# The last stage's down projection by seven half-width products instead of eight full ones, with the next token group's transposes ahead of it

## The chip, the core and the metric

The kernel runs on one core of one Trainium2 chip. The metric is the device time of one execution in microseconds. A profile of one execution comes with it: for every engine (PE is TensorE, PEld its weight loads, DVE is VectorE, ACT is ScalarE, POOL is GpSimd, SP is SyncE, whose queue issues most transfers) it has each instruction's start, duration, and what it waited for.

## The reference, cut to what matters

Two transformer layers on 2048 tokens (2 sequences of 1024) of width 512, in float32. Each of four sublayers is normalised before and after and added to the stream `x`. Only the fourth is touched:

```python
def _L1_ffn_ref(x, w_gate, w_up, w_down):          # widths: 512 -> 2048 -> 512
    h = silu(einsum('bsh,hi->bsi', x, w_gate)) * einsum('bsh,hi->bsi', x, w_up)
    h_sparse = _sparsify_2to4(h)                   # of each 4 neighbours the 2 largest in size stay
    return einsum('bsi,ih->bsh', h_sparse, w_down)

x = x + _layernorm(_L1_ffn_ref(_layernorm(x), w_gate, w_up, w_down))
```

The first sublayer is a small attention over heads of the same token, the second a feed-forward layer with ternary weights, the third causal attention with rotary positions.

## The kernel before

The stream `x_sb` stays on chip: 16 tiles of 128 tokens by 512. The fourth sublayer, called the last stage here, is the code from L1104 to L1304. It goes over the tokens in NG = 4 groups `g` of GW = 512 tokens (four tiles, `GT = 4`), and in each group over NS = 4 slices `S` of the 2048 hidden columns, 512 columns each. A slice is two units `u` (L1192).

**A unit** (`f1_unit`, L1128) computes 256 hidden columns of gate and of up for the group's 512 tokens. Each of the two is a matrix product cut into 2 x 2 blocks and done with seven block products in place of eight (Strassen's scheme in Winograd's form). A block product is two matmuls of 128 x 128 weights against 128 x 256 moving values, so a unit has 2 x 7 x 2 = 28 matmuls. They stand in four phases: eight matmuls, eight, eight, four. ACT copies finished block products out of PSUM, DVE adds others (`add`, L1125); banks come from a ring of eight (`ring8`, L88), six for each unit, so the first bank of a unit is one that a DVE `add` of the unit before has to leave. Between the phases DVE does the preceding unit's work: `multiply` (L1175, two 128x1024 products, after ACT's sigmoid), and a share of the preceding slice's `choice` (L1205: twelve comparisons, additions and masked products that apply the two-of-four rule; `choose(2)`, `choose(3)`, `choose(2)` take the next so many of them).

The token side of the scheme needs sums of blocks of the transposed, normalised tokens; `sides` (L936) makes them in four DVE instructions. The weight side is made on POOL by `derive` (L919) during the first group, four POOL instructions of 128x256 for each of gate and up in each of eight units; all seven blocks are written to DRAM (`kept`), and the later groups load them back whole (`load_unit`, L900, 896 KB each).

**The down projection** (`f1_out`, L1239) of a 128-token tile is 16 matmuls, 128x128 of the hidden values against 128x512 rows of `wd`, in one PSUM bank. `wd` (4 MB) is loaded once, in four pieces during the first group, and stays. A tile's result is normalised and added to the stream (`f1_store`, L1247, through `ln_residual`, L209: statistics on DVE, square root on ACT, scaling on DVE, addition and the store on POOL).

The order of the work in the last stage is written out by hand for PE, ACT, DVE and SP; POOL's is left to the framework. At the end of a group stand: the last unit's sigmoid, `multiply` and the last slice's `choice`; the next group's normalisation (`f1_norm`, L1252); slices 0 to 2 of the first two tiles' down projection, then their slice 3; the next group's transposes (`f1_xT`, L1262, 16 PE transposes) and `sides`; then the other two tiles.

## Time and profile before

| | us |
|---|---|
| median of 3 runs | 1582.63 |
| the runs | 1582.63, 1578.23, 1583.45 |
| profiled execution, its own time | 1577.97 |
| its span, first to last instruction | 1575.8 |
| last stage's first matmul starts | 954.22 |
| last stage's last matmul ends | 1567.39 |

In the profile's rows "f32" matmuls stand as two instructions each, so the 256 down-projection matmuls appear as x512 and a unit's 28 as 56. A "mean ns" is one instruction's duration with its pipeline; back to back they start closer together than that, so the time that a series takes is read from starts. A "windows" row gives, for a stretch, the busy time of each engine and the number of instructions in brackets.

### The profile page before, as it was taken

Reading aid. Unit: us, or ns where it says so; the run is one execution under the profiler, and the core shown is the slowest. Engines: PE = TensorE matmul, PEld = TensorE weight load, DVE = VectorE, ACT = ScalarE, POOL = GpSimd, SP = SyncE. Lnnn points to the kernel's source line nnn. Section 1 sums busy time; section 2 is a strip of 40 time slices with the busy share of each in tenths; the row PEclk is TensorE's granted clock in tenths of the full one; section 3 lists DMA queues with packets and bytes.
Section 4 is the critical chain, followed back from the end, with each engine's and each line's share of the span. In section 5 each row is a group of like instructions: output and inputs, shape, how many; then the busy total and the mean of one; then the engine's idle time right before and its main releaser. Section 6 shows DMA issues by size and latency. Waiting matters only on the chain.

```text
span 1575.8 us, 19277 instructions
## 1 busy us (share of the span) xinstructions
PE 1493.5 (95%) x6614; PEld 977.9 (62%) x6614; DVE 952.7 (60%) x2221; ACT 740.2 (47%) x1876; POOL 304.2 (19%) x382
## 2 busy tenths in 40 slices
PE   6999999999688998998999999999999999999997
PEld 3558787877455544444444447874887488648863
DVE  6886356433676677657667636984377346824761
ACT  4243344322286767896787973440343044204420
POOL 1112335232201211114212015811000100010001
PEclk9999999999879999998899999999999999999999
DMA  7200001011552322225120005760233024203200
GB/s 287 74 1 0 1 1 44 11 34 34 131 135 60 88 50 55 61 54 177 51 54 1 1 1 179 276 233 21 101 141 139 20 109 173 100 21 146 95 1 27
DMA packets 59290, 125.51 MB, mean 80 GB/s; under 512 B 8116, under 2 KB 29622, under 8 KB 59192
## 3 DMA queue, kind: packets, MB, share of 16 engines
q1 hardware_dynamic: 54552, 104.09, 21.4%
q0 software_dynamic: 3584, 18.88, 3.1%
q10 hardware_dynamic: 1056, 1.31, 0.2%
q8 instruction: 52, 0.85, 0.2%
q14 instruction: 46, 0.38, 0.1%
HBM read 94.90 MB, written 29.36 MB: 79 GB/s over the span
## 4 chain that ended last, share of the span: by engine, by line
PE 46%; issue 32%; DVE 9%; ACT 9%; POOL 3%; DMA 1%; SPq 0%; POOLq 0%; ACTq 0%; DVEq 0%
PE ph L366 9%; ACT junk L757 5%; PE po L385 5%; PE pq L243 3%; PE pst L818 3%; PE pq L483 3%; PE psc L742 3%; PE po L847 3%; DVE mxs L753 3%; PE py L863 3%; ACT pT L831 2%; PE po L1242 2%; PE pb_g L1120 1%; PE pb_u L1120 1%; PE pkv L488 1%
## 5 line engine op out<-in xcount | busy, mean ns | idle before, releaser
L753 DVE TENSOR_REDUCE mxs<-psc 128x1 f32<-128x512 f32 (+3 forms) x384 | 196.3, 551 | 90.0 <-PE psc L748 51.0
L757 ACT ACTIVATE junk<-psc,mxs 128x512 bf16<-128x512 f32 (+3 forms) x384 | 222.9, 638 | 26.3 <-DVE mxs L753 18.2
L1242 PE MATMUL po<-wd,h 128*128 128x512 f32 x512 | 220.9, 592 | 0.0
L831 ACT ACTIVATE pT<-pst 128x512 f32<-128x512 f32 (+3 forms) x384 | 160.9, 560 | 54.0 <-PE pst L825 53.6
L366 PE MATMUL ph<-xTg,w 128*128 128x512 f32 x704 | 170.2, 395 | 1.9 <-DVE xTg L356 0.9
L1242 PEld LDWEIGHTS po<-wd,h 128*128 128x128 f32 x512 | 97.0, 190 | 119.3 <-issue 116.5
L742 PE MATMUL psc<-k,q 128*128 128x512 f32 (+3 forms) x384 | 144.0, 448 | 15.5 <-ACT junk L757 9.3
L366 PEld LDWEIGHTS ph<-xTg,w 128*128 128x128 f32 x704 | 132.3, 189 | 30.2 <-DVE xTg L356 1.2
L818 PE MATMUL pst<-q,k 128*128 128x512 f32 (+3 forms) x384 | 125.4, 417 | 11.3 <-ACT junk L757 9.8
L742 PEld LDWEIGHTS psc<-k,q 128*128 128x128 f32 x384 | 75.7, 208 | 78.3 <-ACT pT L831 33.7
L214 POOL TENSOR_TENSOR x_sb<-x_sb,tmp_f 128x512 f32<-128x512 f32 x16 | 20.2, 1260 | 508.4 <-DVE tmp_f L194 508.4
L833 POOL TENSOR_SCALAR_AFFINE_SELECT pT<-pT 128x256 f32<-128x256 f32 x128 | 52.1, 414 | 294.9 <-ACT pT L831 292.9
L818 PEld LDWEIGHTS pst<-q,k 128*128 128x128 f32 x384 | 69.0, 199 | 58.3 <-ACT junk L757 35.3
L757 ACT ACTIVATION_READ_ACCUMULATOR junk<-psc,mxs 128x1 f32 x384 | 100.7, 263 | 0.0
L177 ACT ACTIVATE rs_f<-mv_f,eps_t 128x1 f32<-128x1 f32 (+1 forms) x20 | 5.9, 295 | 200.6 <-DVE mv_f L175 200.6
L847 PE MATMUL po<-pT,v 128*32 128x512 f32 (+3 forms) x768 | 91.6, 513 | 1.6 <-POOL pT L833 1.1
L375 POOL TENSOR_TENSOR hl<-h,hl 128x512 fp32r<-128x512 f32 x44 | 57.1, 1298 | 169.5 <-ACT hl L374 169.5
L385 PE MATMUL po<-w,hl 128*128 128x512 f32 x352 | 87.4, 391 | 1.9 <-DVE tmp L194 1.9
L372 DVE TENSOR_TENSOR h<-h,ph 128x512 f32<-128x512 f32 x44 | 30.0, 684 | 96.4 <-PE ph L366 95.4
L1176 DVE TENSOR_TENSOR gate<-gate,ab 128x1024 f32<-128x1024 f32 x32 | 40.6, 1270 | 77.1 <-ACT ab L1173 77.1
L174 DVE BATCH_NORM_STATS2 st_f<-po 128x6 f32<-128x512 f32 x16 | 11.2, 699 | 108.8 <-PE po L1242 108.8
L385 PEld LDWEIGHTS po<-w,hl 128*128 128x128 f32 x352 | 65.8, 188 | 17.0 <-DVE tmp L194 3.6
(236 smaller groups left out, 2731.6 us busy)
## 6 DMA issues: line engine op xcount, KB each, us to landing
w<-kept SPq DMA_DIRECT2D x48, 896.0 KB, 5.2
q<-dq SPq DMA_DIRECT2D x64, 256.0 KB, 5.0
kept<-w POOLq DMA_DIRECT2D x16, 896.0 KB, 6.6
dq<-hl SPq DMA_DIRECT2D x32, 320.0 KB, 3.0
raw_w<-in_f_w SPq DMA_DIRECT2D x8, 704.0 KB, 8.7
x_sb<-in_x SPq DMA_DIRECT2D x16, 256.0 KB, 5.3
k<-dq SPq DMA_DIRECT2D x16, 256.0 KB, 6.2
w<-in_f_wg SPq DMA_DIRECT2D x8, 512.0 KB, 3.6
```

What stands on the lines that cost most here:

```text
L243: nc.tensor.matmul(pa[:, :n], xT[:, c, :], w[:, c, :], start=(c == 0), stop=False)
L366: nc.tensor.matmul(pa, wt[:, c, cols], xT[:, s, c, :], start=(c == 0 and s == 0), stop=(c == DC - 1 and s == 1),)
L375: nc.gpsimd.tensor_tensor(hl[:, 1, :], h, hl[:, 0, :].bitcast(F32), ALU.subtract)
L385: nc.tensor.matmul(pos0[g][k], hl[:, s, k * P : (k + 1) * P], w3[:, hc, :], start=(hc == 0 and s == 0), stop=(hc == HC - 1 and s == 1),)
L742: nc.tensor.matmul(pa[:, :w], tk.q.bitcast(F32R)[:, r, ii * P : (ii + 1) * P], st.k[ch].bitcast(F32R)[:, g, :w], start=True, stop=True,)
L753: nc.vector.tensor_reduce(mx, pa[:, :w], AX.X, ALU.max, negate=True)
L757: nc.scalar.activation(junk[:, :w], pa[:, :w], AF.Exp, bias=mx, accum_out=tk.sm[:, ii, r, ch : ch + 1])
L818: nc.tensor.matmul(pas[r][:, c0:], st.k[j // GT].bitcast(F32R)[:, g, (j % GT) * P : (j % GT + 1) * P], tk.q.bitcast(F32R)[:, r, c0:], star ...
L831: nc.scalar.activation(p[:, e, c0:], pas[2 * pr + e][:, c0:], AF.Exp)
L833: nc.gpsimd.affine_select(out=p[:, :, c0 : c0 + P], in_=p[:, :, c0 : c0 + P], compare_op=ALU.is_ge, fill=0.0, base=0, pattern=[[0, 2], [1, ...
L847: nc.tensor.matmul(tk.po[DK * r : DK * r + DK, c0:], st.v[j // GT][:, j % GT, g * DK : (g + 1) * DK], tk.pT[j, r // 2][:, r % 2, c0:], sta ...
L1242: nc.tensor.matmul(po, hs[S][:, j, k * P : (k + 1) * P], wd[:, 4 * S + j, :], start=(S == 0 and j == 0), stop=(S == NS - 1 and j == 3),)
```

## The change

**The down projection** is cut 2 x 2 as well: within a slice, its 512 hidden columns into two halves, its 512 output columns into two halves of 256, and the group's tokens into two halves of 256 (tiles 0 and 1 against 2 and 3). Seven block products stand in place of eight. One of the two tile pairs `k` (tiles k and k + 2) takes 7 x 2 = 14 matmuls of 128x128 against 128x256 in each slice. The seven sums of a pair are collected over all four slices in four PSUM banks, two of them side by side in a bank's halves, so both pairs fill all eight banks.

- `token_sums` makes the scheme's four sums of the hidden values on DVE, 128x512 each. Slice 0's are appended to the items that run between phases of slice 1 and 2's units; the other slices' stand after the last unit.
- `load_down`, `derive_down`: the weights of a slice come in two rotating buffers of seven blocks. In the first group the four derived blocks of slices 0 and 1 are made on POOL during the last slice's units, those of slices 2 and 3 on DVE; they are written to DRAM. Later groups load three blocks from the input (768 KB) and four from there (1024 KB). Slices 2 and 3 can only be loaded when the products of slices 0 and 1 have left the buffer.
- `f1_collect` puts a pair's seven sums together: one ACT copy, four DVE instructions.
- Statistics of a result use the DVE-only inverse root (`inverse_root`, 13 small instructions, which `ln_stats(roots=False)` had inside) and no square root on ACT, but for the very last pair. The first pair's are done at once; those of the second pair are put among the next group's first units.
- The next group's normalisation moves from the end of the group into slice 2's units, and its scaling from DVE to ACT in slice 3's. The transposes now stand directly after the last unit, ahead of the down projection.
- `choose()` takes a share of the waiting items by an assumed duration instead of a count. `ab` has one buffer instead of two. POOL's order in the last stage is now the written one.
- Of the gate and up blocks only the four that differ from the input are written to DRAM (512 KB instead of 896) and loaded back in two transfers (384 KB from the input, 512 KB).

```diff
 def load_unit(n):
-    nc.sync.dma_start(out=w, in_=kept[n % NU, i])
+    nc.sync.dma_start(out=w[:, 0:3]..., in_=src[n % NU][:, : 6 * P])
+    nc.sync.dma_start(out=w[:, 3:7], in_=kept[n % NU, i])
...
+def load_down(g, S):
+    w = w1b.tile([P, 7, 2, HW], F32, tag="wd7", name=f"wd7_{g}_{S}", bufs=2)
+    if g == 0:
+        nc.sync.dma_start(out=w[:, 0:4]..., in_=f1_wd[S])
+        raw_down[S] = w
+    else:
+        nc.sync.dma_start(out=w[:, 0:3]..., in_=f1_wd[S][:, : 3 * D])
+        nc.sync.dma_start(out=w[:, 3:7], in_=kept_down[S])
+    down[g, S] = [w[:, k] for k in range(7)]
+
+def derive_down(S, eng):
+    w = raw_down.pop(S)
+    b11, b21, b22, b12, t1, t2, t4 = (w[:, k] for k in range(7))
+    eng.tensor_tensor(t1, b12, b11, ALU.subtract)
+    eng.tensor_tensor(t2, b22, t1, ALU.subtract)
+    eng.tensor_tensor(b12, b22, b12, ALU.subtract)
+    eng.tensor_tensor(t4, b21, t2, ALU.subtract)
+    kept_down[S] = dw.tile([P, 4, 2, HW], F32, tag="keptd", name=f"keptd_{S}", bufs=NS)
+    nc.gpsimd.dma_start(out=kept_down[S], in_=w[:, 3:7])
...
+def choose(all=False):
+    share = sum(w for w, _ in chain) / max(1, slots[0])
+    slots[0] -= 1
+    while chain and (all or share > 0.2):
+        w, f = chain.pop(0)
+        f()
+        share -= w
...
 def f1_hidden(g, S, B, then):
-            if g == 0 and u == 1:
-                nc.sync.dma_start(out=wd[:, 4 * S : 4 * S + 4, :], in_=...)
+            if S < 2 and u == 1:
+                load_down(g, S)
+            if g == 0 and S == NS - 1:
+                derive_down(u, nc.gpsimd)
...
+def token_sums(g, S, h):
+    x = s2.tile([P, 3, 2, HW], F32, tag="hx", name=f"hx_{g}_{S}")
+    a11, a12 = h[:, 0:2, :HW], h[:, 2:4, :HW]
+    a21, a22 = h[:, 0:2, HW:], h[:, 2:4, HW:]
+    ...
+    (x[:, 0], a21, a22, ALU.add), (x[:, 1], x[:, 0], a11, ALU.subtract),
+    (a21, a11, a21, ALU.subtract), (x[:, 2], a12, x[:, 1], ALU.subtract),
...
+def f1_down(g, S, k, acc):
+    pairs = ((a11, b11), (s1_, t1), (a12, b21), (s2_, t2), (s4_, b22), (s3_, t3), (a22, t4))
+    for m, (a, b) in enumerate(pairs):
+        for j in range(2):
+            start = S == 0 and j == 0 and m % 2 == 0
+            nc.tensor.matmul(
+                acc[m // 2][:, m % 2 * HW : (m % 2 + 1) * HW],
+                a[:, j, k * P : (k + 1) * P], b[:, j, :],
+                start=start, stop=True, skip_group_check=not start,
+            )
...
+def f1_collect(nm, acc):
+    nc.scalar.copy(p15, halves(acc[0]))
+    nc.vector.tensor_tensor(halves(o[:, 0, :]), halves(acc[1]), p15[:, 0:1, :].to_broadcast(two), ALU.add)
+    nc.vector.tensor_tensor(e, halves(acc[2]), o[:, 0:1, HW:].to_broadcast(two), ALU.add)
+    nc.vector.tensor_tensor(o[:, :, HW:], e, p15[:, 1:2, :].to_broadcast(two), ALU.add)
+    nc.vector.tensor_tensor(o[:, 1, :HW], acc[3][:, :HW], e[:, 1, :], ALU.add)
...
-            choose(len(chain))
-            if more:
-                xns = f1_norm(g + 1)
-            po = [ring8(f"po1_{g}_{k}") for k in range(2)]
-            for k in range(2):
-                f1_out(k, hs, po[k], range(NS - 1))
-            for k in range(2):
-                f1_out(k, hs, po[k], [NS - 1])
-                f1_store(g, k, po[k])
-            if more:
-                B = f1_xT(g + 1, xns)
-            for k in range(2, GT):
-                ...
+            choose(all=True)
+            end.sigmoid()
+            if more:
+                xT, xd = f1_xT(g + 1, xns)
+            end.multiply()
+            end.size()
+            run(token_sums(g, 1, hs[1]))
+            choose(all=True)
+            if more:
+                B = sides(xT, xd)
+            acc = [[ring8(f"acc_{g}_{k}_{m}") for m in range(4)] for k in range(2)]
+            for S in range(NS):
+                if S >= 2:
+                    run(token_sums(g, S, hs[S]))
+                    if g == 0:
+                        derive_down(S, nc.vector)
+                for k in range(2):
+                    f1_down(g, S, k, acc[k])
+                    if g == NG - 1 and S == k == 0:
+                        nc.scalar.activation(warm, eps_t, AF.Sqrt)
+                    if S == NS - 1:
+                        f1_store(g, k, f1_collect(f"{g}_{k}", acc[k]), more and k == 1, g == NG - 1 and k == 1)
+                if S < 2:
+                    load_down(g, S + 2)
```

## The prediction

> **What bounds the kernel now.** I read the page's busy shares first, then the windows of the last stage cut at its units of work, then PE's waits there, and the timeline for the rates and the end.

> ```profile
> PE 1493.5 (95%) x6614; PEld 977.9 (62%) x6614; DVE 952.7 (60%) x2221; ACT 740.2 (47%) x1876; POOL 304.2 (19%) x382
> ...
> L1242 PE MATMUL po<-wd,h 128*128 128x512 f32 x512 | 220.9, 592 | 0.0
> ```

> TensorE is busy 95% of the span, and the products to be changed (L1242) hold it 220.9 us with no idle time before them. PE's waits between 940 us and the end have one line:

> ```profile
> PE pb_g L1120 <- DVE gate L1126: 0.8, 1, 0.8
> ```

> So the last stage, 954.22 to 1567.39 us, is bound by PE to within a microsecond. The averages hide how near DVE is behind it. Windows of one unit (12.1 us) each, the first five in the first group (units 3 to 7, counted from 0), the last two in the second:

> ```profile
> core 0: us, PE busy (x) PEld busy (x) DVE busy (x) ACT busy (x) POOL busy (x), PEclk, DMA share, GB/s
> 990.50:1002.60 12.10, 12.10 (x57) 10.43 (x55) 12.07 (x16) 5.39 (x12) 10.99 (x13) 1.00 0.88 324
> 1002.60:1014.70 12.10, 11.25 (x53) 9.81 (x53) 11.76 (x14) 5.15 (x11) 9.50 (x12) 1.00 0.73 277
> 1014.70:1026.80 12.10, 12.10 (x58) 10.65 (x57) 12.07 (x16) 5.32 (x12) 11.31 (x11) 1.00 0.91 307
> 1026.80:1038.90 12.10, 12.10 (x57) 10.50 (x56) 11.35 (x16) 5.53 (x12) 2.62 (x4) 1.00 0.84 288
> 1038.90:1051.00 12.10, 12.10 (x58) 10.65 (x57) 8.99 (x20) 5.52 (x12) 0.00 (x0) 1.00 0.64 238
> ...
> 1145.10:1157.20 12.10, 12.10 (x58) 10.65 (x57) 8.99 (x18) 5.53 (x12) 0.00 (x0) 1.00 0.41 152
> 1157.20:1169.30 12.10, 12.10 (x58) 10.65 (x57) 8.74 (x13) 5.53 (x12) 0.00 (x0) 1.00 0.40 153
> ```

> The third figure is DVE's. In later groups it has 3.2 us free in a unit. In the first group the same work fills it (12.07 of 12.10) while POOL derives weights, and the 0.85 us that PE lacks in the second row is the wait above. DVE is the second bound, in the first group alone.

> **The change, part by part.**

> *Products removed and added.* PE's rates, from starts (the first two lines are units, the last two the old down projection):

> ```profile
> 1200.32 1.03 PE L1120 MATMUL pb_g<-xTg,w 128*128 128x256 f32 x4
> 1201.19 1.03 PE L1120 MATMUL pc_g<-xTg,w 128*128 128x256 f32 x4
> ...
> 1555.17 0.19 PEld L1242 LDWEIGHTS po<-wd,h 128*128 128x128 f32 x1 [0.24 <-issue]
> ...
> 1566.33 0.19 PEld L1242 LDWEIGHTS po<-wd,h 128*128 128x128 f32 x1 [0.24 <-issue]
> ```

> A unit's 28 matmuls take 12.08 us (1193.42 to 1205.50 in the timeline): 0.4315 us each. The old ones start an instruction each 0.429 us (26 steps from 1555.17 to 1566.33), and a matmul is two: 0.8585 us. A group had 64 of these, 54.95 us; it gets 4 slices x 2 pairs x 14 = 112 of 128x256, the form of the units, 48.33 us. That is 6.62 us a group, 26.5 us in four. Weight loads rise from 512 to 896 instructions of 0.19 us; in the units they lie under products of just this width, so nothing more is counted.

> *The transposes* (16, from 1232.97 to 1234.72, 1.75 us) are only moved. They and slice 0's products (12.1 us) now cover what follows the last unit. From its end DVE has about 1.2 us of leftover choice, sigmoid until 1.5, `multiply` 2.4, slice 1's sums 2.7: ready near 6.6 us; PE wants them at 1.75 + 12.1 = 13.8. Then the last choice (8.4, from 1210.73 to 1219.10), `sides` 3.0 and slice 2's sums 2.7: near 21 us, wanted at 25.9. Slice 3 is wanted at 38. In the first group two derivations (2.7 us each) come between, and still fit. No stall; if DVE is over 5 us late here, slice 2 stalls first.

> *Weights.* Four 1 MB loads go. In the first group four 1 MB loads and four 1 MB stores come, later two loads a slice. Those of slices 2 and 3 are issued when the preceding slice's products end, so one slice of products (12.1 us) has to cover each; SP's issues behind them (the next group's units) then leave up to 26 us later than now, but are used 50 us later. Rows that are near:

> ```profile
> w<-kept SPq DMA_DIRECT2D x48, 896.0 KB, 5.2
> ...
> wd<-in_f_wd SPq DMA_DIRECT2D x4, 1024.0 KB, 12.6
> ```

> 1792 KB on queues that are otherwise still is a pair of the first row, about 7 us; the second row was queued behind unit loads. I take 7, hidden; 12.6 for a part is the other end, and a rival below. The unit loads, now split, carry the same bytes and have two units' time. The smaller `kept` stores only relieve.

> *Result.* Pair 0: ACT copy 0.7, four DVE instructions 2.6, statistics 2 x 0.8, inverse root 2.4 (13 instructions, 1222.42 to 1224.80), scaling 1.0: 8.3 us. Pair 1's products are 6.0 us, so its collection starts 2.3 us after the last product. Between groups the next unit takes pair 0's banks first; pair 1's are wanted 4 and 6 us into it and free by then: nothing. At the very end it is paid. Before:

> ```profile
> 1567.39 0.70 DVE L174 BATCH_NORM_STATS2 st_f<-po 128x6 f32<-128x512 f32 x1 [11.37 <-PE po L1242]
> ...
> 1569.84 1.25 POOL L214 TENSOR_TENSOR x_sb<-x_sb,tmp_f 128x512 f32<-128x512 f32 x1 [11.62 <-DVE tmp_f L194]
> 1571.39 0.56 POOL L1250 DMA_DIRECT2D out<-x_sb  x1 [0.30 <-POOL x_sb L214]
> ```

> From 1567.39 to the span's end, 8.4 us, 4.7 of them after POOL's addition. After: 2.3 wait, 2.6 collection, 1.6 statistics, 0.75 for root, reciprocal and mean, 0.65 scaling, 1.3 addition, 4.7: 13.9. Cost 5.5 us, once.

> *DVE inside the units.* Two units of a later group hold choice 8.4, `multiply` 4.8, adds 4.0. While slice 1's units run, slice 0's sums come in (2.6): 19.8 of 24.2. While slice 2's and part of slice 3's run, normalisation comes in (four statistics 3.2, root 2.4, mean 0.2 = 5.8): 23.0 of 24.2. It fits with 1 us to spare; the scaling on ACT (5.5 us busy of 12.1) is free. I count 0, bounds 0 and 3 us for each of two groups, since items are not cut evenly.

> In the first group nothing is free. Added there: sums 2.6, normalisation 5.8, and POOL's eight derivations of 128x512 (1.26 us each by the row of L214, 10 us) beside DVE in slice 3's units. What POOL takes from DVE: from 984 to 1031 us DVE needs some 45 us for work that takes 32 in later groups (two choices, three `multiply`, four units' adds: 16.8 + 7.2 + 8), beside 32 POOL instructions that take 0.73 each when undisturbed (23.4 us): 0.55 of POOL's time. So 10 us cost 5.5. [...] The rows say about half, and they are this kernel's mix, so I take 5.5 and keep 10 for the range. Sum 2.6 + 5.8 + 5.5 = 13.9. Against it stand DVE's free 3.9 us in slice 3's units (rows four and five) and some 1.5 us that may run over behind the last product: 8.5 us of PE stalls, placed at the starts of slice 2's second and slice 3's first unit, where `add` has to leave a bank. [...] if the derivations fall into pauses, 3.

> *Nothing else*: 15 fewer square roots with table loads on ACT were hidden; stages before 954 us keep their order on PE, DVE and ACT.

> **Sum**: -26.5 + 5.5 + 8.5 = -12.5. The profiled execution took 1577.97, so 1565.5 on its scale. That run lies below all three timed ones; against their median, 1582.63, it is 1570.1, which I forecast.

> **Rivals.**

> 1. *DVE's extra work finds room.* For it: PE stalled only 0.85 us with DVE at 99.8%. Against: that DVE had no gap left in which to put 8.5 us. Then -26.5 + 5.5 = -21: 1561.6.

> 2. *DVE binds in every group with normalisation.* For it: 23.0 of 24.2, and two instructions of statistics directly ahead of the adds that free a bank. Then 3 us in two groups and 12 in the first: 1582.63 - 26.5 + 5.5 + 6 + 12 = 1579.6. Half of such cases still end over 5 us faster.

> 3. *The reloaded slice comes late.* Six waits (two in each later group) for a transfer that now can't start early. Beyond 12.1 us each microsecond of landing costs 6; from 14.2 us the gain of 12.5 is gone. Were the two parts together to land in 17.5 us (12.6 and a part again), 6 x 5.4 = 32 us: 1602. Against: the pair of 896 KB, and a queue without other loads at that time.

> 4. *Half-width products cost more than width says.* The units' rows at 0.4315 exclude it.

> **How the numbers follow.** My forecast 0.53, rival 1 0.22, rival 2 0.17, rival 3 0.08. What this kernel's timing can tell from no change is about 0.3%, 4.75 us. Faster: 0.50 of the forecast's 0.53, all of 0.22, half of 0.17: 0.80. Same 0.10, slower 0.10. The range takes rival 1 with 3 us of run-to-run spread below, 1558, and reaches into rival 2 to 1580; left out are rival 3, and a part of 2. The forecast's own range is 1564 to 1576.

> **What would show it.** In the profile after: 896 instructions of the down projection with starts 0.216 us apart; about 146.7 us from one later group to the next in place of 153.4; PE waits for DVE `gate` of some 8.5 us in all, all before 1060 us; DVE at 12 of 12.1 us from slice 1 to slice 3 of the first group; span end some 14 us after the last product; no PE wait for a down-projection weight. Wrong would be: PE waits for DVE in later groups over 2 us each (rival 2), waits for SP's weights (rival 3), or a first group without stalls (rival 1).

## The result, and the profile after

The changed kernel takes 1573.54 us (median of 11 runs), the kernel before 1582.63 beside it: a ratio of 0.9941 with a 95% interval of 0.9924 to 0.9958, that is 9.1 us less. The forecast was 1570.1, with a range of 1558 to 1580.

The lines of the page that answer to those shown of before, from the profiled execution (span 1571.8 us, time 1573.54):

```profile
PE 1473.6 (94%) x6998; PEld 1054.4 (67%) x6998; DVE 1027.6 (65%) x2393; ACT 742.2 (47%) x1877; POOL 317.7 (20%) x392
...
L1315 PE MATMUL acc<-wd,h 128*128 128x256 f32 x512 | 121.6, 379 | 0.0
...
L1315 PE MATMUL acc<-wd,hx 128*128 128x256 f32 x384 | 93.3, 379 | 0.0
```

PE has lost 19.9 us of busy time, DVE has gained 74.9. The down projection is now 896 instructions and waits for nothing. (The busy figures of the two rows sum to 214.9 us, while 896 starts, 0.215 us apart as below, fill 192.6: the starts of the timeline are the safer reading.) The timeline of PE, first product of the last stage, the transposes of groups 1 and 2, and two rows at the end:

```profile
960.75 1.03 PE L1160 MATMUL pb_g<-xTg,w 128*128 128x256 f32 x4
...
1071.10 1.91 PE L212 MATMUL ptf<-ident,xnf 128*128 128x128 f32 x16
1217.88 1.91 PE L212 MATMUL ptf<-ident,xnf 128*128 128x128 f32 x16
...
1556.36 1.89 PE L1315 MATMUL acc<-wd,hx 128*128 128x256 f32 x8
1558.08 1.89 PE L1315 MATMUL acc<-wd,h 128*128 128x256 f32 x8
```

Eight starts take 1.72 us, 0.215 each. From transposes to transposes a later group takes 146.78 us; before it took 153.37 (1079.60 to 1232.97). The gain of the products is there in full, 6.59 us a group, 26.4 in four. What is missing was lost in the first group. PE's waits in the last stage (columns: in total, times, longest):

```profile
PE pc_g L1160 <- DVE gate L1166: 3.5, 1, 3.5
PE pb_g L1160 <- ACT gate L1208: 2.4, 1, 2.4
PE pb_g L1160 <- DVE gate L1166: 2.0, 2, 1.8
```

They sum to 7.9 us, against one of 0.8 before, and all lie before 1056 us. But the first group is longer than its waits tell: from its first product to the next transposes it takes 110.35 us, where a later group takes 96.69, so 13.66 us more. Nearly all of the rest is in the first figure behind the engines in the windows, PE's granted clock (PEclk). Every change of it in this trace, 31 in all, lies a whole number of steps of 3.413 us from every other, so the windows are cut at these steps; here they are around the two longest waits:

```profile
core 0: us, PE busy (x) PEld busy (x) DVE busy (x) ACT busy (x) POOL busy (x), PEclk, DMA share, GB/s
1036.17:1039.58 3.41, 0.65 (x4) 0.22 (x2) 3.38 (x5) 0.37 (x1) 3.09 (x4) 1.00 0.94 292
1039.58:1042.99 3.41, 2.65 (x6) 2.19 (x7) 3.38 (x7) 0.00 (x0) 3.33 (x4) 0.50 0.94 370
1042.99:1046.41 3.42, 3.42 (x9) 2.70 (x8) 3.28 (x6) 1.96 (x4) 3.02 (x4) 0.50 0.31 128
1046.41:1049.82 3.41, 3.41 (x17) 3.00 (x16) 3.34 (x5) 0.75 (x2) 3.41 (x3) 1.00 0.47 192
...
1053.23:1056.65 3.42, 1.16 (x5) 1.06 (x6) 2.90 (x4) 1.59 (x3) 0.00 (x0) 1.00 0.19 79
1056.65:1060.06 3.41, 3.41 (x9) 2.71 (x9) 3.39 (x7) 0.88 (x3) 0.00 (x0) 0.50 0.67 227
```

After the wait of 3.5 us PE runs at half its clock for 6.1 us (2.65 and 3.42), after the one of 2.4 us for 3.4 us: nine instructions in a step instead of seventeen. Half of those 9.5 us is lost: 4.75 us that no list of waits shows.

One measure is used below beside the medians: the stretch from the last stage's first product to the end of the span. The start of that stage differs from run to run (954.22 and 958.25 us in two profiles of the kernel before), the stretch does not: 621.58 and 621.65 us. It was 611.05 us in the changed kernel, 10.5 less. It comes from one profile each, and what a half clock adds to it belongs to that profile (see the last section).

| kernel | first group over a later one | PE waits in the units | products at half clock in the units | stretch | median | ratio to before |
|---|---|---|---|---|---|---|
| before | 1.2 | 0.85 | 0 | 621.6 | 1582.63 | |
| changed | 13.66 | 7.9 | 9.5 | 611.05 | 1573.54 | 0.9941 |
| normalisation in slice 0 | 13.2 | 10.0 | 3.4 | 610.6 | 1568.82 | 0.9926 |
| derivation on DVE | 8.7 | 5.6 | 3.2 | 606.1 | 1565.62 | 0.9899 |
| normalisation and sums moved | 11.7 | 6.9 | 6.8 | 609.2 | 1572.91 | 0.9943 |
| the same, short tail | 12.0 | 7.2 | 6.8 | 607.7 | 1570.16 | 0.9918 |
| statistics in slice 0 | 10.8 | 7.0 | 5.7 | 608.2 | 1569.72 | 0.9933 |
| statistics in slice 0, derivation on DVE | 5.4 | 4.4 | 0 | 602.9 | 1562.31 | 0.9900 |
| all moved, short tail | 4.4 | 3.2 | 0 | 606.7 | 1570.52 | 0.9942 |
| all moved, second version | 5.6 | 3.1 | 3.4 | 601.75 | 1565.35 | 0.9898 |

The second column is the start of group 1's transposes less the start of the stage, less 96.69; for the kernel before, whose transposes stand elsewhere, it is from first product to first product, 154.59 us less 153.38. Take the waits and half of the fourth column from it, and 0.8 to 1.5 us are left in all nine changed kernels: the two explain nearly all of the excess. The ratio is to the kernel before as it ran beside that kernel; its median there was 1582.63, 1582.52, 1579.67 or 1582.24, so medians of different rows can differ by 3 us for that reason alone.

### The profile page after: what moved, and what is told of

The parts are those of the page before. It is cut to its first block, busy times and chain, and to the rows that moved or that the text cites. A ratio compares the mean times of both kernels' runs of the same rounds, so it can differ in the third digit from the quotient of the medians.

```text
span 1571.8 us, 20347 instructions
## 1 busy us (share of the span) xinstructions
PE 1473.6 (94%) x6998; PEld 1054.4 (67%) x6998; DVE 1027.6 (65%) x2393; ACT 742.2 (47%) x1877; POOL 317.7 (20%) x392
## 3 DMA queue, kind: packets, MB, share of 16 engines
q10 hardware_dynamic: 1056, 1.31, 0.3%
## 4 chain that ended last, share of the span: by engine, by line
PE 73%; DVE 13%; ACT 8%; issue 3%; POOL 1%; DMA 1%; SPq 0%; POOLq 0%; ACTq 0%; DVEq 0%
PE acc L1315 12%; PE ph L371 9%; PE pb_g L1160 6%; PE pb_u L1160 6%; ACT junk L762 5%; PE po L390 5%; PE psc L747 3%; PE pq L488 3%; PE pq L248 3%; PE pst L823 3%; PE po L852 3%; PE pc_g L1160 3%; PE pc_u L1160 3%; PE py L868 3%; DVE mxs L758 3%
## 5 line engine op out<-in xcount | busy, mean ns | idle before, releaser
L823 PE MATMUL pst<-q,k 128*128 128x512 f32 (+3 forms) x384 | 123.1, 410 | 12.1 <-ACT junk L762 10.4
L1315 PE MATMUL acc<-wd,h 128*128 128x256 f32 x512 | 121.6, 379 | 0.0
L1315 PEld LDWEIGHTS acc<-wd,h 128*128 128x128 f32 x512 | 97.0, 190 | 13.1
L1363 POOL TENSOR_TENSOR x_sb<-x_sb,o 128x512 f32<-128x512 f32 x14 | 19.2, 1374 | 427.2 <-DVE o L199 427.1
L1315 PE MATMUL acc<-wd,hx 128*128 128x256 f32 x384 | 93.3, 379 | 0.0
L1315 PEld LDWEIGHTS acc<-wd,hx 128*128 128x128 f32 x384 | 73.0, 190 | 9.9
L1332 ACT COPY p<-acc 128x512 f32<-128x512 f32 x8 | 4.7, 586 | 157.7 <-PE acc L1315 157.7
## 6 DMA issues: line engine op xcount, KB each, us to landing
wd<-keptd SPq DMA_DIRECT2D x12, 1024.0 KB, 9.5
```

The costliest lines, as they stand in the source:

```text
L823: nc.tensor.matmul(pas[r][:, c0:], st.k[j // GT].bitcast(F32R)[:, g, (j % GT) * P : (j % GT + 1) * P], tk.q.bitcast(F32R)[:, r, c0:], star ...
L1315: nc.tensor.matmul(acc[m // 2][:, m % 2 * HW : (m % 2 + 1) * HW], a[:, j, k * P : (k + 1) * P], b[:, j, :], start=start, stop=True, skip_g ...
```

## The experiments

**First theory**: DVE has too much to do in the first group's units, so spreading its work over them frees PE. **Rival**: it is POOL's work beside DVE's, wherever the work stands.

### Normalisation in slice 0's units

```
+            if g == 0:
+                xns, norm, scales = f1_norm(1)
+                fill(norm, 6)
...
-                    if S == 1 and more:
+                    if S == 1 and more and g > 0:
```

> Edit: the changed kernel, with group 1's normalisation (its 16 statistics, the inverse root and the two scalings) put into the units of slice 0 of the first group instead of those of slice 1. Nothing else moves; slice 0's units held 8.5 us of VectorE work in 12.1 us slots, so there is room for about 3.5 us a unit there, and slices 1 to 3 lose the surplus. Theory (VectorE has too much to do in the first group's units while GpSimd derives the down weights[...]): of the 7.9 us of TensorE waits in the first group under 3 are left, the granted clock stays 1.00 through slices 2 and 3, the first group lasts about 152 instead of 160.4 us, and the time falls by 6 to 9 us, to about 1566. Rival (it is GpSimd's derivation of the down weights beside VectorE's small instructions that makes the waits, wherever the normalisation stands): waits move but over 5 us of them stay, and the time changes by less than 3 us.

Measured: 1568.82 us, ratio 0.9926 (0.9899 to 0.9953). The median of four runs is 4.7 us below the changed kernel's, but the stretch, which leaves the earlier stages out, is only 0.5 us shorter, and the waits rose to 10.0 us. The two longest waits of PE in this kernel, then the first and last instruction of the inverse root on DVE with one from between, and one of POOL's at that time:

```profile
PE pb_g L1160 <- POOL w L937: 3.1, 1, 3.1
PE pb_g L1160 <- ACT gate L1208: 2.5, 1, 2.5
```

```profile
977.54 0.69 DVE L188 TENSOR_SCALAR nv_f1n<-mv_f1n 128x4 f32<-128x4 f32 x1
...
979.76 0.65 DVE L194 TENSOR_TENSOR nv_f1n<-nv_f1n 128x4 f32<-128x4 f32 x1
...
984.24 0.16 DVE L206 SCALAR_TENSOR_TENSOR nb<-mv_f1n,rs_f1n 128x4 f32<-128x4 f32 x1
984.32 0.41 DVE L1166 TENSOR_TENSOR gate<-gate,pa_g 128x256 f32<-128x256 f32 x1
...
979.66 0.73 POOL L937 TENSOR_TENSOR w<-w 128x256 f32<-128x256 f32 x1
```

The inverse root works on 128x4 numbers and is over in 2.5 us when POOL is still (next run). It took 6.9 here, since many of its instructions lasted 0.6 to 0.7 us, as long as POOL's subtraction of 128x256 beside them, and one lasted 1.2. The addition behind it left its bank at 984.73, and PE went on at 984.84. The line calls POOL's `w` the releaser, but that had ended at 984.19; DVE's addition was later and fits. So moving the root brought it beside other POOL instructions, and the waits moved with it. That is the rival's reading.

### Down weights derived on DVE

```
-                derive_down(u, nc.gpsimd)
+                derive_down(u, nc.vector)
```

> Edit: the changed kernel, with the down weights of slices 0 and 1 derived by VectorE instead of GpSimd, in the same units; the keeping of the weights and GpSimd's issue of it stay. It gives VectorE 8 more subtractions of 128x512 (about 0.6 to 1.2 us each, so some 5 to 9 us) in the first group and takes GpSimd's 1.3 us instructions away from beside VectorE's small ones. Rival (GpSimd's instructions, which the small VectorE instructions wait out, are the cause): the inverse root lasts 2.8 instead of 7 us, VectorE's pass is no slower than in a later group, the waits fall below 4 us and the time falls by 4 us or more. Theory (it is the sum of the work that is too much for VectorE, from whichever side it comes): the first group's waits stay between 6 and 12 us, the time is within 3 us of the changed kernel's or above it.

Measured: 1565.62 us, ratio 0.9899 (0.9875 to 0.9923), stretch 4.9 us shorter. DVE does 5.5 us of work more, and the kernel is faster. The root in the changed kernel, with one of POOL's subtractions and the copy that PE waited 2.4 us for:

```profile
1044.57 1.69 DVE L188 TENSOR_SCALAR nv_f1n<-mv_f1n 128x4 f32<-128x4 f32 x1
...
1048.87 1.20 DVE L194 TENSOR_TENSOR nv_f1n<-nv_f1n 128x4 f32<-128x4 f32 x1
...
1048.78 1.26 POOL L1138 TENSOR_TENSOR wd<-wd 128x512 f32<-128x512 f32 x1
...
1055.09 0.35 ACT L1208 COPY gate<-pb_g 128x256 f32<-128x256 f32 x1
```

The root with the derivation on DVE, with the first subtraction behind it, and then PE's waits in the last stage:

```profile
1040.39 0.17 DVE L188 TENSOR_SCALAR nv_f1n<-mv_f1n 128x4 f32<-128x4 f32 x1
...
1042.77 0.16 DVE L206 SCALAR_TENSOR_TENSOR nb<-mv_f1n,rs_f1n 128x4 f32<-128x4 f32 x1
1042.85 0.68 DVE L1135 TENSOR_TENSOR wd<-wd 128x512 f32<-128x512 f32 x1
```

```profile
PE pc_g L1160 <- DVE gate L1166: 3.5, 1, 3.5
PE pb_g L1160 <- DVE gate L1166: 2.1, 1, 2.1
```

The root is back at 2.5 us; in the changed kernel it lasted from 1044.57 to 1051.55, and `multiply`, ScalarE's `Abs` and the copy stood behind it. That wait is gone (2.4 us), and of the 9.5 us of products at half clock 3.2 are left, worth 3.1 us less. The time went as the rival said, but the waits did not fall under 4 us: the 3.5 us wait is untouched, so it has another cause.

### Normalisation and token sums moved

```
+                    if S == 2 and g == 0:
+                        return ops + token_sums(g, 0, hs[0])
```

> Edit: as the kernel with the normalisation in slice 0's units, and the first group's token sums (its second-tile sums for slice 0) put into slice 3's units instead of slice 1's. It spreads VectorE's work of the first group nearly evenly over its four slices. Theory (too much VectorE work in single units): the first group's TensorE waits fall below 1.5 us, its length to 147 to 150 us, the granted clock stays 1.00, and the time is 9 to 12 us below the changed kernel's, near 1562. Rival (the excess of the first group is the cost of fetching and deriving the weights for the first time, and no order of VectorE's work frees it): the first group stays above 155 us and the time within 4 us of the changed kernel's.

Measured: 1572.91 us, ratio 0.9943 (0.9919 to 0.9967), stretch 1.9 us shorter. DVE's work is now spread over all four slices, and the first group is still 11.7 us too long: waits of 3.0 us behind the root in slice 0, again beside POOL's instructions, and of 2.0 us at slice 3, with 3.4 us of half clock behind each. The first theory falls as it was stated: spreading DVE's work was not enough. The numbers are those of this run's rival (the first group lasts 158.5 us), but that fetching and deriving the weights for the first time costs so much in any order is refuted below, where the group lasts 152.2 and 152.4 us.

### The same with a shorter tail

Shown is the line on additions and stores; ScalarE's square root for both last pairs comes with it.

```
-            for i, eng, queue in ((0, nc.vector, nc.sync), (1, nc.gpsimd, nc.gpsimd)):
+            for i, eng, queue in ((0, nc.vector, nc.sync), (1, nc.vector, nc.scalar)):
```

> Edit: as the kernel with normalisation and token sums both moved, and the tail shortened: the inverse root of both last output pairs by ScalarE's square root, both additions of x on VectorE instead of one on GpSimd, and the two last stores issued by SyncE and ScalarE. In the changed kernel the tail from the last product's end to the span's end was 11.8 us, with GpSimd's addition of 1.31 us and its issue of 0.56 us in its chain. Theory: the tail falls to about 10 us, the first group lasts 147 to 150 us, and the time is 11 to 14 us below the changed kernel's, near 1560. Rival (the last store's own landing and the collection set the tail, so that the engine doesn't matter): the tail stays within 0.7 us of 11.8 and the time is that of the kernel with the two moves alone.

Measured: 1570.16 us, ratio 0.9918 (0.9895 to 0.9940). From the last product's end to the end of the span it takes 10.2 us instead of 11.9: the tail gave 1.7 us, as expected; the first group kept its excess.

### A square: who derives, and where the statistics stand

The 3.5 us wait is for the addition at 1039.79, ahead of which the changed kernel's DVE has two scalings of the hidden slice and two statistics (1.7 us, from 1038.19):

```profile
1035.89 2.37 DVE L1280 SCALAR_TENSOR_TENSOR h<-sb,h 128x512 f32<-128x512 bf16 x2
...
1039.79 0.40 DVE L1166 TENSOR_TENSOR gate<-gate,pc_g 128x256 f32<-128x256 f32 x1
```

So the four statistics of group 1 went into slice 0's units, with the root left where it was, once with the derivation on DVE and once on POOL.

```
+            if g == 0:
+                xns, norm, scales = f1_norm(1)
+                fill(norm[:-1], 6)
+                norm = norm[-1:]
```

On DVE: 

> Edit: as the kernel that derives the down weights of slices 0 and 1 on VectorE, and of group 1's normalisation the four statistics (3.4 us of VectorE) stand in slice 0's units while its inverse root stays where the changed kernel has it, in slice 3's first unit, when GpSimd has ended its derivations. Theory (the inverse root's small instructions are slow only beside GpSimd's instructions, and what is left is VectorE's backlog at slice 3's first unit, of which two of the statistics are 1.7 us): the inverse root lasts 2.5 us, the 3.5 us wait becomes 1 to 2 us, the clock stays 1.00, TensorE's waits in the first group sum to 3 to 4 us, and the time falls by about 3 us below the kernel with the derivation on VectorE, to 1562 or 1563. Rival (the 3.5 us wait is set by the scalings of the hidden slice and the conversion of the group's weights, not by the statistics): the wait stays at 3 us or more and the time within 1.5 us of 1565.6.

Measured: 1562.31 us, ratio 0.9900 (0.9876 to 0.9924). PE's waits, and two steps of the clock around the end of the one of 2.0 us:

```profile
PE pc_g L1160 <- DVE gate L1166: 2.0, 1, 2.0
PE pb_g L1160 <- DVE gate L1166: 1.8, 1, 1.8
PE pb_g L1160 <- ACT gate L1208: 0.6, 1, 0.6
```

```profile
1031.26:1034.68 3.42, 1.59 (x8) 1.44 (x9) 3.38 (x9) 0.67 (x3) 0.77 (x2) 1.00 0.85 263
1034.68:1038.09 3.41, 3.41 (x17) 3.03 (x16) 3.03 (x15) 1.88 (x4) 0.00 (x0) 1.00 0.94 360
```

The clock stays at 1.00, and the first group's excess (5.4) is its waits (4.4) and 1.0 us more. In the changed kernel the same difference was 5.8: the half clock is what lies between. The root lasted 2.5 us, as expected. The median is the 1562 that was expected, but by luck of the sitting: the kernel before was 2.9 us faster there than beside the derivation on DVE alone, and the ratio is the same (0.9900 and 0.9899). What the statistics gave shows in the profile only.

On POOL: 

> Edit: the changed kernel, with the four statistics of group 1's normalisation in slice 0's units and its inverse root where it was; the down weights of slices 0 and 1 are derived by GpSimd as in the changed kernel. It is the fourth corner of a square whose other corners lasted, from the last stage's first product to the end, 611.05 us (changed kernel), 606.11 (derivation on VectorE) and 602.86 (derivation on VectorE, statistics in slice 0). Theory (two separate costs: statistics ahead of the addition that frees a bank, worth the 3.25 us between the last two, and the inverse root beside GpSimd's subtractions, worth the rest): 607 to 608.5 us; the root lasts 6 to 7 us; the wait for ScalarE's copy (2.4 us in the changed kernel) stays and the 3.5 us wait falls to about 2. Rival (only the sum of VectorE's work in slices 2 and 3 counts, so that the statistics alone give it room enough): the wait for ScalarE's copy is gone and the stretch is 603 to 604.5 us.

Measured: 1569.72 us, ratio 0.9933 (0.9910 to 0.9956). The stretches of the four corners are 611.05 and 608.2 us with POOL deriving, 606.1 and 602.9 with DVE. POOL's derivation costs 4.9 or 5.3 us, the place of the statistics 2.9 or 3.2. More than half of POOL's part and about half or more of the other is half clock: without it (4.75, 2.85, 1.6 and 0 us in the four) POOL's derivation costs 1.8 or 2.5 us and the place of the statistics 1.0 or 1.6, as an estimate from single profiles. The ratios bear out the first (0.9941 against 0.9899, whose intervals do not overlap; 0.9933 against 0.9900, whose do), not the second (0.9941 against 0.9933, 0.9899 against 0.9900). The stretch came as the theory said and the root lasted 6.8 us, but the single waits did not: the wait at slice 3 grew to 4.6 us and the one for ScalarE's copy shrank to 1.0. DVE at that place, and POOL's subtractions beside it:

```profile
1036.14 3.41 DVE L1280 SCALAR_TENSOR_TENSOR h<-sa,h 128x512 f32<-128x512 bf16 x2
1039.47 1.75 DVE L1280 SCALAR_TENSOR_TENSOR h<-sb,h 128x512 f32<-128x512 bf16 x1
1041.14 0.41 DVE L1166 TENSOR_TENSOR gate<-gate,pc_g 128x256 f32<-128x256 f32 x1
1041.47 1.15 DVE L1166 TENSOR_TENSOR gate<-gate,p 128x256 f32<-128x256 f32 x1
...
1039.07 1.60 POOL L1136 TENSOR_TENSOR wd<-wd 128x512 f32<-128x512 f32 x1
1040.63 1.71 POOL L1137 TENSOR_TENSOR wd<-wd 128x512 f32<-128x512 f32 x1
```

With the statistics gone from there, the scalings met POOL's long subtractions: 1.75 us for one that takes 0.68 when POOL is still. The addition that reads a PSUM bank took its 0.41, the one of two operands in SBUF 1.15 instead of 0.41.

### Everything moved, in two versions

The token sums go to slice 3, slice 1's down weights are derived on DVE in the product phase, and the tail is the short one. In the first version that derivation stands behind everything else that DVE does after the units.

```
-            if g == 0 and S == NS - 1:
-                derive_down(u, nc.vector)
+            if g == 0 and S == NS - 1 and u == 0:
+                derive_down(0, nc.vector)
...
-                    if g == 0:
-                        derive_down(S, nc.vector)
+                if g == 0 and S >= 1:
+                    derive_down(S, nc.vector)
```

> Edit: as the kernel with the statistics in slice 0 and the down weights derived on VectorE; in addition the first group's token sums for slice 0 in slice 3's units instead of slice 1's, the derivation of slice 1's down weights in the product phase instead of slice 3's second unit, and the shortened tail (ScalarE's square root for both last pairs, both additions of x on VectorE, the last stores issued by SyncE and ScalarE). Theory (what is left is the backlog of VectorE up to slice 3[...]): the first group's waits sum to under 1.5 us, its length is 147 to 149 us, the tail 10.2 us, and the time about 1560, or 13 us below the changed kernel's. Rival (VectorE binds wherever its work is put, since its sum in the group is unchanged): over 4 us of waits stay and the time is 1564 or above.

Measured: 1570.52 us, ratio 0.9942 (0.9920 to 0.9964). The units were nearly free, but PE's longest wait is now in the products:

```profile
PE acc L1315 <- DVE wd L1135: 4.2, 1, 4.2
...
1082.37 2.08 PE L1315 MATMUL acc<-wd,hx 128*128 128x256 f32 x4 [4.19 <-DVE wd L1135]
```

DVE came to that derivation at 1081.63, 18.3 us after the transposes began, and the products ran at half clock to 1085.8. Neither side of the expectation had named this place. In the second version the derivation stands directly behind slice 1's token sums:

```
             run(token_sums(g, 1, hs[1]))
+            if g == 0:
+                derive_down(1, nc.vector)
```

> Edit: as the kernel with everything moved, but slice 1's down weights are derived directly behind slice 1's token sums instead of behind the choice of slice 3 and the conversion of the next group's input; there VectorE reached it only 18.6 us after the last unit, and TensorE waited 4.2 us for it and ran at half clock for 3.4 us after. Theory: that wait goes and nothing takes its place, the first group's waits sum to 3.2 us, none above 2 us, the clock stays 1.00, and from the last stage's first product to the end it lasts 600.5 to 602 us instead of 606.7 (611.05 in the changed kernel); time about 1561. Rival (VectorE's work behind the last unit is as tight as in the units, so that the conversion now comes late for the next group or the choice for slice 3's products): a new wait of 2 us or more in the product phase, and 604 us or more.

Measured: 1565.35 us, ratio 0.9898 (0.9881 to 0.9916); stretch 601.75 us, as expected and the shortest of all. Waits, and the step of the clock that holds the first, with the step behind it:

```profile
PE pb_g L1160 <- DVE gate L1166: 2.1, 1, 2.1
PE pb_g L1160 <- ACT gate L1208: 0.6, 1, 0.6
PE pc_g L1160 <- DVE gate L1166: 0.5, 1, 0.5
```

```profile
1008.58:1011.99 3.41, 1.36 (x7) 0.88 (x6) 3.41 (x8) 0.37 (x1) 2.33 (x4) 1.00 0.91 294
1011.99:1015.40 3.41, 3.41 (x10) 2.66 (x9) 1.84 (x3) 1.70 (x3) 3.26 (x4) 0.50 0.48 193
```

"The clock stays 1.00" was wrong: a wait of 2.05 us was enough here. Between this version and the one with statistics in slice 0 and the derivation on DVE the medians decide nothing (ratios 0.9898 and 0.9900 to before); both are faster than the changed kernel, by 8 to 9 us in the stretch.

### The reload doubled

```
             nc.sync.dma_start(out=w[:, 3:7], in_=kept_down[S])
+            nc.sync.dma_start(out=w[:, 3:7], in_=kept_down[S])
```

> Edit: the changed kernel, with the kept part (1024 KB) of each reloaded slice of down weights fetched twice into the same place in groups 1 to 3; 12 MB more are moved in all. In the changed kernel the kept part landed 9.5 us after its issue, and the slice is needed 12.1 us after the buffer came free. The prediction's third rival decided from a landing of 14.2 us. If that cover is what the trace says: the last landing comes at 15 to 19 us, TensorE waits 1 to 5 us for a down weight at each of the six reloads, 6 to 30 us in all. If the reload is hidden by more than that (the buffer comes free earlier than the count says): no wait for a down weight, and the later groups still last 146.8 us.

One profiled execution: 1576.30 us, stretch 611.12 us against 611.05. No wait for a down weight. SyncE's issues for slice 2 of group 1:

```profile
1234.60 0.33 SPq L1124 DMA_DIRECT2D wd<-in_f_wd  x1
1234.98 0.43 SPq L1127 DMA_DIRECT2D wd<-keptd  x1
1241.50 0.32 SPq L1128 DMA_DIRECT2D wd<-keptd  x1
```

The third was issued at 1241.50, and the second had landed 6.5 us after its issue, at 1241.48; so the first two were in place 6.9 us after the first issue. The third took 5.2 us more in this stretch: 12.1 us in all, just what the cover allows. The changed kernel's own reloads whose landing the trace holds took 7.0, 7.1 and 8.4 us from the first issue, so some 4 to 5 us are to spare. The expectation's 15 us was too high, as it took the page's median of 9.5 us; that median mixes these reloads (kept part 6.7, 6.7 and 8.0 us in the changed kernel) with the ones issued among unit loads (two of them 11.0 and 11.4).

### The kernel before, once more

> Edit: none; the kernel before, profiled a second time. In its first profile the last stage began at 954.2 us, in the changed kernel's at 960.8 and in four variants of it between 956.2 and 958.1, with the same order of TensorE's work up to there. If the start differs from run to run through the granted clock: it lies at 956 to 961 here. If the change delays the stages ahead of the last: it stays at 954 to 955.

One profiled execution: 1582.08 us; the last stage began at 958.25 us, 4 us later than in the first profile. So the start varies by itself; what sets it was not followed. In ten profiles of the changed kernel and its variants it lay between 955.4 and 963.5 us, 959.4 on average. Whether the change delays the earlier stages by a microsecond or two on average can't be told from two profiles of before.

## Why the prediction was right, point by point

The forecast of a gain, by its own likeliest case, held; the median came 3.4 us above it. Against the stretch (the gain of 12.5 us came out as 10.5), the terms are as follows; two of them were off in opposite directions (the tail 2.1 us too dear, the first group some 4 us too cheap), so that the total came nearer than its parts, which is luck:

- *Products, -26.5.* Measured -26.4 (four times 6.59). The step from the units' rate of 0.4315 us to the down projection was exact, and rival 4 was rightly excluded.
- *The tail, +5.5.* Measured +3.4: 11.8 us from the last product's end, against 8.4 before. The mis-sized term is the 2.3 us that pair 1's collection was to wait for pair 0. In the trace pair 0 was through at 1559.88 and pair 1's collection began at 1559.79, before PE's last matmul ended: pair 0's additions had started bank by bank, the first at 1551.48, while its own last products still ran. The remaining steps, 11.6 by the prediction, were right.
- *Stalls in the first group, +8.5.* The waits rose by 7.1 us (7.9 less the 0.85 of before), near the places named: 1.8 us at the start of slice 2's first unit (its second was named), the rest in slice 3's first unit. DVE was full there as foreseen, 12.0 of 12.1 us in each unit from slice 1's second to the end of slice 2. But the consequence was left out: the half clock after the two longest, 4.75 us. This is the largest step that was missing. The first group's excess rose from 1.2 to 13.66 us, 12.45 instead of 8.5, of which waits and half clock are 11.85. The terms sum to -26.4 + 3.4 + 7.1 + 4.75 = -11.15; the stretch says -10.5, and the 0.6 us between lies in the first group too, its cause open.
- *What POOL takes from DVE.* The prediction took 5.5 of POOL's 10 us and kept 10 for its range; that all of it might be lost, no row of before shows. In the changed kernel POOL's eight subtractions last 10.5 us, and the DVE instructions beside them are 6.3 us longer than their undisturbed forms (four of the root 4.5, two additions 1.7). With the statistics moved it is 8.9 of 11.1. The single rows differ: with the statistics moved, the addition with an operand in PSUM took its 0.41 us beside POOL, the one of two SBUF operands 1.15. The root's first instruction, of one input, was lengthened too (1.69 us instead of 0.17 in the changed kernel), the statistics there, also of one input, were not (0.66 to 0.68); why, no run here shows. "About half" was a mean over a mix, not a rate: the loss depended on which DVE instructions stood there. In the changed kernel each of the root's four long instructions ended 0.02 to 0.04 us after one of POOL's subtractions (the first at 1046.26 after 1046.22, the last at 1050.07 after 1050.04), so that the chain of tiny ones took 7.0 us, and it was this, ahead of `multiply`, that made the 2.4 us wait. The prediction placed no wait there.
- *Later groups, 0.* 146.78 us against 146.7. Rival 2 is refuted: in a later group no wait of PE is listed, and DVE is busy 103.7 of 146.8 us.
- *The reload, hidden at 7 us.* Measured 6.9 to 8.4 in a product phase; twice the kept part just fitted into 12.1. Rival 3 had more margin than its chance of 0.08 suggested.
- *The transposes, covered.* No wait in the products behind them. The margin is not large: one derivation more, put at the end of DVE's work there, cost 4.2 us.

That DVE's work would find room (rival 1) is refuted for this order of work, but nearly true of another: with statistics, sums and derivations placed away from POOL's instructions, 3.1 us of waits remained.

## What to carry to other kernels

Before giving POOL a job beside a busy DVE, look at which DVE instructions will run then. Here ones of 128x4 lasted up to 1.69 us beside POOL's subtractions of 128x512 instead of 0.17, and an addition of two operands in SBUF 1.15 instead of 0.41; it was cheaper to let the busy DVE do the job itself, by 4.9 or 5.3 us of the stretch. When an order is tight, read the granted clock behind each TensorE wait: here a wait of 2.05 us within one step of the clock cost 1.7 us more and one of 3.5 us in the changed kernel 3 more, and the list of waits does not contain that. Two profiles of this kernel that differ by 1.7 us, half of a step of 3.413, may differ only in how a wait lay on the clock's steps. Compare small changes in one stage by the stretch of that stage, when earlier stages vary from run to run.

## What was not expected of the hardware

```profile
1006.97:1010.39 3.42, 1.74 (x8) 1.56 (x9) 3.42 (x7) 0.41 (x2) 1.84 (x4) 1.00 0.94 271
1010.39:1013.80 3.41, 3.41 (x18) 3.00 (x17) 3.34 (x4) 2.34 (x5) 3.19 (x3) 1.00 0.42 171
```

The waits of 2.50 us (normalisation in slice 0, divided into 1.04 and 1.46) and 2.03 us (statistics in slice 0 with derivation on DVE, 0.20 and 1.83) cost no clock either, with less than 1.935 us in each step, and one of 1.94 us within a step (normalisation and sums moved, short tail) did. The drop came at the end of the step, 2.3 to 4.2 us after the wait began. The 1.935 us holds for these products only: in earlier stages the clock also fell after steps with as little as 0.32 us of idle time (650.84 to 654.26 in the kernel before). And it is read off traces; no run placed a wait on the steps on purpose.

*Tiny DVE instructions as long as POOL's big ones.* 128x4 operations of 0.16 us took 0.6 to 0.7 us (once 1.2) beside POOL's 128x256 and 1.1 to 1.7 us beside its 128x512. The statistics, reading 128x512 from SBUF as their one input, took 0.66 to 0.69 us with or without POOL.
